# Reads of turned rows and of x, cut into 128-partition transfers instead of 32-partition ones, in a fused adaptive-layer-norm transformer block

## The chip, the cores and the metric

The kernel runs on one core of a Trainium2 chip. The metric is the device time of one execution in microseconds (us). Before the change it is 3508.1 us, the median of three runs (3507.44 to 3511.53). The engines are named as in the profile: PE is TensorE, PEld its weight loads, DVE is VectorE, ACT is ScalarE, POOL is GpSimd, SP is SyncE, which here issues nearly all DMA transfers.

## The reference

All tensors are float32. For each of 8 batch elements, x has 1024 tokens of 512 values. Causal attention with 16 heads of 32 values is followed by a GELU layer of 2048, both with a modulation that depends on a condition vector:

```
mod = silu(cond) @ Wada + bada                       # 6 rows of 512 per batch element
sh_a, sc_a, gt_a, sh_m, sc_m, gt_m = split(mod, 6)
xm = layernorm(x, g1, be1) * (1 + sc_a) + sh_a
x  = x + gt_a * (causal_attention(xm, Wqkv) @ Wproj + bproj)
xm = layernorm(x, g2, be2) * (1 + sc_m) + sh_m
x  = x + gt_m * (gelu(xm @ W1 + b1) @ W2 + b2)
```

What the change touches lies between the layer norm and the first product after it: the normalized rows (tokens in the partitions) have to be turned, so that the 512 features lie in the partitions, because a product on TensorE sums over partitions.

## The kernel before

The 8192 tokens are worked on as 16 blocks of 512 tokens (two per batch element). Each block has a first stage (key `a0` to `a15`, normalization of x ahead of the projections to queries, keys and values) and a second stage (`m0` to `m15`, normalization ahead of the GELU layer). The products are cut by a Strassen scheme into seven half-size products over the parts B11, B21, B22 and T1 to T4 of the modulated, turned activations `xm` (`strassen`). Attention of one block is interleaved with projections and the GELU layer of others.

The order of the instructions on each engine is written out by the program itself: a planner keeps an estimated clock per engine (`now`) and due times of tiles (`written`, `left`), and picks at each step which thread of work advances. The cost that it books for a DMA is an argument of `note_dma`: 3600 ns for each transfer of x, 2600 ns for the write of a turned block to DRAM and 1250 ns for each read back. At run time the engines follow that fixed order, each in turn, and wait on semaphores. Transfers are all issued by SP in a fixed order: weight tiles of 256 KB into a ring of eight buffers (`fetch`, lines 358 to 362), x, residual rows, outputs, and the turn.

A turn happens in two ways. The keys in `by_pe` (a0, a1, m0, m1, m14, m15) are turned by TensorE, through transposes against an identity (line 764). The other 26 keys (a2 to a15 and m2 to m13) go through DRAM:

- `load_x` (lines 402 to 414) reads a block of x into the tile `hat_a`, 128 partitions by 4 by 512 values. For turned keys the token that stands in partition 32m + i at place a is token (4m + a) * 32 + i of the block. Four transfers of 256 KB fill the tile. `x` rows are 2 KB.
- `normalize` takes the statistics of each quarter `tiles[:, t, :]` (line 619) on DVE, a power on POOL, and applies mean and deviation to each quarter on ACT or DVE (lines 655 and 660).
- `turn` (lines 692 to 716) transposes 32 by 32 blocks of each quarter on DVE (line 700), with the modulated tile `xm` as a scratch place, writes this tile to DRAM as `held` in one transfer of 1 MB (line 709), waits for it, and reads it back in four transfers of 256 KB into the `hat` tile (lines 712 to 715), where now the features lie in the partitions.
- `modulated` (lines 721 to 789) then makes four chunks of `xm`, each from all four quarters `got[:, :, ts(c, P)]`, with a scale and a shift on ACT (line 774) or DVE (line 768), and the sums and differences T1 to T4 on DVE and POOL (lines 784 to 789 and 167, 170). TensorE's products read `xm_a`, `xm_m` and their sums `t_a`, `t_m` (line 217).

The same ACT queue holds the exponentials of the attention (line 1698) and evacuations of product banks (line 197); DVE holds the row maxima (line 1610) and the other evacuations (line 208).

Of the kernel before, what the change touches and what calls it, by code (L numbers as in the profile page):

```python
# [22 lines left out]
def kernel(  # L23
# [33 lines left out]
    nc = tc.nc  # L57
    B, T, D = x.shape
    HD = W1.shape[1]
    P = 128  # L60
    hd = D // H
    scale = float(hd) ** -0.5
    TB = 512
    NTT = TB // P
# [48 lines left out]
    def note(engine, ns, reads=(), writes=(), port=False):  # L113
        start = max(now[engine], due(reads, writes))
        if port:
            start = max([start] + [b for a, b in pool_spans if a <= start < b])
        end = start + ns
        now[engine] = end
        if engine == "POOL":
            pool_spans.append((start, end))  # L120
            del pool_spans[:-16]
        for k in reads:
            left[k] = max(left.get(k, 0.0), end + SYNC)
        for k in writes:
            written[k] = end + SYNC
        return end

    def note_dma(ns, reads=(), writes=(), after=0.0):

        begun = max(now["SP"], due(reads, ()), after)  # L130
        now["SP"] = begun + ISSUE
        now["DMA"] = max(begun + BEGIN, now["DMA"]) + ns
        for k in writes:
            written[k] = now["DMA"] + LAND
# [108 lines left out]
    def mlp_steps(n):  # L243
        return [("u", n, i) for i in range(NQ)] + [("d", n, part) for part in range(4)]
# [9 lines left out]
    for w in range(1, NB):  # L254
        n = w - 1
        m = mlp_steps(n)
# [132 lines left out]
    rows = tmp.tile([P, TB], F32, tag="y", name="rows")[:n_rows, :P]  # L389
# [8 lines left out]
    Q = P // NTT  # L398

    def hat_tile(key):  # L400
        return tmp.tile([P, NTT, D], F32, tag="hat", name=f"hat_{key}", bufs=1)

    def load_x(n):
        b, h = blocks[n]
        rows = hat_tile(f"a{n}")
        written["hat free"] = NEVER
        for t in range(NTT):
            some = x[b, h * TB + t * P : h * TB + (t + 1) * P, :]
            if f"a{n}" in by_pe:
                nc.sync.dma_start(rows[:, t, :], some)  # L410
            else:
                nc.sync.dma_start(rows[ts(t, Q), :, :], some.rearrange("(t i) d -> i t d", i=Q))
            note_dma(3600, [], [("x", f"a{n}")])
        return rows

    x_pre = {0: load_x(0)}
    fetch()

# [134 lines left out]
    def add_job(job, reads, first=False):  # L553

        at = sum(1 for other in jobs if other[2]) if first else len(jobs)
        jobs.insert(at, (job, reads, first))
# [135 lines left out]
    def turn(key, rows, xm):  # L692

        small_blocks = xm.rearrange("p c n -> p (c n)")
        by_tile = small_blocks.rearrange("p (m h t i) -> p h m t i", m=NTT, h=NC, t=NTT)
        written["blocks", key] = NEVER

        def turn_tile(t):
            into = by_tile[:, :, :, t, :]
            nc.vector.transpose(into, rows[:, t, :].rearrange("p (h m i) -> p h m i", m=NTT, i=Q))  # L700
            done = [("blocks", key)] if t == NTT - 1 else []
            note("DVE", 620, [("hat", key, t)], done)

        for t in range(NTT):
            add_job(lambda t=t: turn_tile(t), [("hat", key, t)], key[0] == "m")
        yield [("blocks", key)], []
        held = kept.tile([P, NTT * D], F32, tag=f"held_{turns[0] % 2}", name=f"held_{key}")
        turns[0] += 1
        nc.sync.dma_start(held, small_blocks)
        note_dma(2600, [("blocks", key)], [("held", key)])  # L710
        yield [("held", key)], []
        for m in range(NTT):
            some = held[:, ts(m, D)].rearrange("(a i) d -> i a d", i=Q)
            nc.sync.dma_start(rows[ts(m, Q), :, :], some)
            note_dma(1250, [("held", key)], [("turned", key)])
        yield [("turned", key)], []

# [3 lines left out]
    def modulated(key, gain, shift, b, guards):  # L721
# [23 lines left out]
        if turned:  # L745
            yield from turn(key, got, xm)
# [590 lines left out]
    def perform(step):  # L1337
# [7 lines left out]
        elif kind == "columns_m":  # L1345
            columns_of["m"] = norm_columns("m", 3, 4, O_G2, O_BE2)
        elif kind == "load_xa":
            x_pre[step[1]] = load_x(step[1])
        elif kind == "load_xr":
            start(load_xr(step[1]))  # L1350
# [643 lines left out]
```

## Time and profile before

| | us |
|---|---|
| median of three runs | 3508.1 |
| the profiled execution, its own time | 3510.74 |
| its span, from the first to the last instruction | 3509.0 |
| PE busy | 3454.3 (98%) |
| DVE busy | 2198.9 (63%) |
| POOL busy | 2084.2 (59%) |
| ACT busy | 1212.4 (35%) |
| DMA, queue of SP, share of 16 engines | 47.1% |

The granted clock of the profiled execution is 0.998. The profile is of one execution; an instruction is listed by its line in the kernel, its engine, what it writes and reads (out<-in, buffer numbers left out), its shape as partitions x elements, and a count. "Idle before" is the time that the engine stood still just ahead of such instructions, followed by what ended most of it. A row of the chain tells the share of the span by what the end of the work hung on, followed backwards. A DMA queue is listed with its packets, megabytes and the share of the 16 DMA engines' time that the packets took. In a table of stretches, the DMA share is the mean over the 16 engines, and a share a little over 1 comes from packets being booked to the stretch in which they start.

### The profile page before, as it was taken

Reading aid. Unit: us, or ns where it says so; the run is one execution under the profiler, and the core shown is the slowest. Engines: PE = TensorE matmul, PEld = TensorE weight load, DVE = VectorE, ACT = ScalarE, POOL = GpSimd, SP = SyncE. Lnnn points to the kernel's source line nnn. Section 1 sums busy time; section 2 is a strip of 40 time slices with the busy share of each in tenths; the row PEclk is TensorE's granted clock in tenths of the full one; section 3 lists DMA queues with packets and bytes.
Section 4 is the critical chain, followed back from the end, with each engine's and each line's share of the span. In section 5 each row is a group of like instructions: output and inputs, shape, how many; then the busy total and the mean of one; then the engine's idle time right before and its main releaser. Section 6 shows DMA issues by size and latency. Waiting matters only on the chain.

```text
span 3509.0 us, 120365 instructions
## 1 busy us (share of the span) xinstructions
PE 3454.3 (98%) x54429; PEld 1724.0 (49%) x54429; DVE 2198.9 (63%) x2401; ACT 1212.4 (35%) x1276; POOL 2084.2 (59%) x2258
## 2 busy tenths in 40 slices
PE   8999999999999999999999999999999999999999
PEld 4444445445554545445454454544555444554445
DVE  5766676564666656665666566765666756656563
ACT  2335333342233423335223342333423343232531
POOL 3767846666366663756727576275753658537660
PEclk9999999999999999999999999999999999999999
DMA  6843444535545445363454534545354544443334
GB/s 212 263 137 104 137 115 140 142 107 159 142 125 156 119 147 153 119 170 115 137 157 130 155 117 144 150 137 148 116 155 137 165 122 146 128 136 101 96 121 140
DMA packets 328194, 491.10 MB, mean 140 GB/s; under 512 B 27260, under 2 KB 177596, under 8 KB 324100
## 3 DMA queue, kind: packets, MB, share of 16 engines
q1 hardware_dynamic: 327568, 483.39, 47.1%
q8 instruction: 428, 7.01, 0.8%
q14 instruction: 82, 0.67, 0.1%
q10 hardware_dynamic: 116, 0.03, 0.0%
HBM read 425.57 MB, written 55.64 MB: 137 GB/s over the span
## 4 chain that ended last, share of the span: by engine, by line
PE 83%; POOL 7%; DMA 3%; DVE 3%; ACT 1%; issue 1%; SPq 1%; ACTq 0%; DVEq 0%; POOLq 0%
PE bank L217 59%; PE sc L1595 8%; PE st L1686 6%; PE po L1726 6%; POOL pT L1816 4%; PE st L1674 2%; PE bank L1747 2%; DMA hat_m<-held_m 1%; DVE mx L1610 1%; POOL hT L170 1%; ACT pT L1698 1%; DMA held_m<-xm_m 1%; PE bank L1648 0%; POOL xr L170 0%; DMA w<-in_L_cond_Wqkv_dram 0%
## 5 line engine op out<-in xcount | busy, mean ns | idle before, releaser
L1816 POOL TENSOR_TENSOR pT<-pT,pT 128x256 f32<-128x256 f32 (+3 forms) x1254 | 1219.7, 1007 | 298.5 <-PE po L1726 181.6
L1698 ACT ACTIVATE pT<-st 128x2048 f32<-128x2048 f32 x288 | 540.9, 1878 | 1065.1 <-PE st L1686 959.8
L217 PE MATMUL bank<-w,hT 128*32 128x256 f32 x14336 | 823.7, 380 | 0.4 <-issue 0.4
L1610 DVE TENSOR_REDUCE mx<-sc 128x4 f32<-128x2048 f32 (+3 forms) x384 | 665.9, 1755 | 235.6 <-PE sc L1595 229.5
L217 PEld LDWEIGHTS bank<-w,hT 128*32 128x32 f32 x14336 | 446.7, 110 | 390.3 <-issue 105.8
L217 PE MATMUL bank<-xm_m,w 128*32 128x256 f32 x8192 | 498.6, 381 | 3.6 <-ACT xm_m L774 2.2
L217 PE MATMUL bank<-t_m,w 128*32 128x256 f32 x6144 | 382.4, 380 | 0.9 <-DVE t_m L786 0.6
L217 PEld LDWEIGHTS bank<-xm_m,w 128*32 128x32 f32 x8192 | 255.6, 110 | 231.2 <-issue 62.2
L1703 POOL TENSOR_SCALAR_AFFINE_SELECT pT<-pT 128x512 f32<-128x512 f32 x256 | 167.5, 672 | 331.9 <-ACT pT L1698 329.4
L1607 DVE TENSOR_TENSOR sc<-sc,mask 128x1024 f32<-128x1024 f32 (+1 forms) x160 | 162.8, 1018 | 293.3 <-PE sc L1595 237.8
L1595 PE MATMUL sc<-kT,qT 32*128 32x512 f32 (+3 forms) x3072 | 329.5, 521 | 4.3 <-ACT pT L1698 3.3
L1726 PE MATMUL po<-pT,v 128*32 128x512 f32 (+3 forms) x3048 | 301.6, 490 | 3.9 <-POOL pT L1703 3.9
L1686 PE MATMUL st<-qT,kT 32*128 32x512 f32 (+3 forms) x3072 | 300.8, 487 | 0.0
L217 PEld LDWEIGHTS bank<-t_m,w 128*32 128x32 f32 x6144 | 189.6, 110 | 172.9 <-issue 48.5
L1765 DVE RECIPROCAL rec<-rec 128x128 f32<-128x128 f32 x256 | 227.3, 922 | 48.2 <-ACT rec L1756 48.2
L217 PE MATMUL bank<-xm_a,w 128*32 128x256 f32 x3968 | 243.4, 382 | 0.4 <-DMA w<-in_L_cond_Wqkv_dram 0.4
L217 PE MATMUL bank<-w,qT 128*32 128x512 f32 x2048 | 237.0, 595 | 1.1 <-DMA w<-in_L_cond_Wproj_dram 0.7
L1595 PEld LDWEIGHTS sc<-kT,qT 32*128 32x128 f32 x3072 | 129.6, 183 | 188.2 <-issue 88.4
L208 DVE TENSOR_TENSOR hT<-bank,u_u 128x512 f32<-128x512 f32 x187 | 126.6, 686 | 105.8 <-PE bank L217 103.1
L217 PE MATMUL bank<-t_a,w 128*32 128x256 f32 x2944 | 183.2, 380 | 0.0
L217 PEld LDWEIGHTS bank<-xm_a,w 128*32 128x32 f32 x3968 | 123.5, 110 | 110.3 <-issue 29.3
L1115 ACT ACTIVATE hT<-hT,cols 128x512 f32<-128x512 f32 x256 | 164.7, 712 | 35.9 <-DVE hT L208 28.5
(243 smaller groups left out, 3404.0 us busy)
## 6 DMA issues: line engine op xcount, KB each, us to landing
w<-in_L_cond_W_dram SPq DMA_DIRECT2D x384, 256.0 KB
w<-kept_up_S SPq DMA_DIRECT2D x256, 256.0 KB
w<-kept_down_S SPq DMA_DIRECT2D x256, 256.0 KB
w<-kept_qkv_S SPq DMA_DIRECT2D x180, 256.0 KB
w<-in_L_cond_Wqkv_dram SPq DMA_DIRECT2D x147, 256.0 KB
hat_a<-in_x_dram SPq DMA_DIRECT2D x64, 256.0 KB
xr<-in_x_dram SPq DMA_DIRECT2D x32, 512.0 KB
w<-in_L_cond_Wproj_dram SPq DMA_DIRECT2D x64, 256.0 KB
```

Of the source, the lines that this page charges most:

```text
L208: nc.vector.tensor_tensor(out, src, other, op)
L217: nc.tensor.matmul(ps[r, :], columns, rhs, start=start, stop=stop, skip_group_check=True)
L1115: nc.scalar.activation(hT[:, i, :], hT[:, i, :], AF.Gelu, bias=cols[:, O_B1 + f : O_B1 + f + 1])
L1595: nc.tensor.matmul(sc[:, j, c0 : c0 + w], qTs[n][r, gg, ts(qt, P)], keys_of(n, kh)[r, gg, :w], start=True, stop=True, skip_group_check=True,)
L1607: nc.vector.tensor_tensor(place, place, shape_of.to_broadcast(place.shape), ALU.add)
L1610: nc.vector.tensor_reduce(maxima[n, gg][:, kh, qt, :], sc[:, :, c0 : c0 + w], axis=AX.X, op=ALU.max)
L1686: nc.tensor.matmul(st[:, j, c0 : c0 + w], kT[r, gg, ts(k % NTT, P)], qT[r, gg, TB - w :], start=False, stop=True, skip_group_check=True,)
L1698: nc.scalar.activation(pT[:, :, :used], st[:, :, :used], AF.Exp, scale=scale)
L1703: nc.gpsimd.affine_select(diagonal, diagonal, pattern=[[0, HPG], [1, P]], compare_op=ALU.is_ge, fill=0.0, base=0, channel_multiplier=-1,)
L1726: nc.tensor.matmul(po[r, TB - w :], v[:, k % NTT, g * P + j * hd : g * P + (j + 1) * hd], pT[:, j, c0 : c0 + w], start=(k == 0), stop=last ...
L1765: nc.vector.reciprocal(some, some)
L1816: nc.gpsimd.tensor_tensor(into, into, pT[:, j, c0 : c0 + w], ALU.add)
```

## The change

Both the reads of x for turned keys and the reads of turned rows are cut along the other axis of the tile. The tile holds the same values in the same places afterwards, and there are as many transfers of the same size in the same order. Before, transfer t (or m) filled all four places in 32 partitions (four runs of 2 KB in each). Now transfer t (or a) fills one place, one run of 2 KB, in all 128 partitions. On the DRAM side a transfer of x took four runs of 32 consecutive rows that follow one another; now it takes four runs of 32 consecutive rows that are 128 rows apart. For the turned rows, the source was 2 KB from each of the 128 rows of `held`; now it is all 8 KB, in four pieces that go to four partitions, of each of 32 rows. The reads for a0 and a1 stay as they are. The planner's costs stay as they are too.

```diff
         for t in range(NTT):
-            some = x[b, h * TB + t * P : h * TB + (t + 1) * P, :]
             if f"a{n}" in by_pe:
-                nc.sync.dma_start(rows[:, t, :], some)
+                nc.sync.dma_start(rows[:, t, :], x[b, h * TB + t * P : h * TB + (t + 1) * P, :])
             else:
-                nc.sync.dma_start(rows[ts(t, Q), :, :], some.rearrange("(t i) d -> i t d", i=Q))
+                some = x[b, h * TB : (h + 1) * TB, :].rearrange("(m a i) d -> a m i d", a=NTT, i=Q)
+                nc.sync.dma_start(rows[:, t, :], some[t])
             note_dma(3600, [], [("x", f"a{n}")])
...
-        for m in range(NTT):
-            some = held[:, ts(m, D)].rearrange("(a i) d -> i a d", i=Q)
-            nc.sync.dma_start(rows[ts(m, Q), :, :], some)
+        for a in range(NTT):
+            some = held[ts(a, Q), :].rearrange("i (m d) -> m i d", m=NTT)
+            nc.sync.dma_start(rows[:, a, :], some)
             note_dma(1250, [("held", key)], [("turned", key)])
```

Here `P` is 128, `Q` is 32, `NTT` is 4, `D` and `TB` are 512.

## The prediction

> **What bounds the kernel now.** I read the page first: the busy times and the chain, then the DMA queues.
>
> ```profile
> span 3509.0 us, 120365 instructions
> ...
> PE 3454.3 (98%) x54429; PEld 1724.0 (49%) x54429; DVE 2198.9 (63%) x2401; ACT 1212.4 (35%) x1276; POOL 2084.2 (59%) x2258
> ...
> DMA packets 328194, 491.10 MB, mean 140 GB/s; under 512 B 27260, under 2 KB 177596, under 8 KB 324100
> ...
> q10 hardware_dynamic: 116, 0.03, 0.0%
> ...
> PE 83%; POOL 7%; DMA 3%; DVE 3%; ACT 1%; issue 1%; SPq 1%; ACTq 0%; DVEq 0%; POOLq 0%
> ```
>
> TensorE is busy in 98% of the span: 3509.0 less 3454.3 leaves 54.7 us of idle time in all. So a faster transfer can win little and a slower one can cost much, wherever TensorE ends up waiting for it. Next I read what TensorE waits for. The rows give us in total, times, and the longest.
>
> ```profile
> PE bank L217 <- ACT xm_m L774: 2.2, 2, 2.0
> ...
> PE bank L764 <- ACT xm_a L774: 1.2, 1, 1.2
> ...
> PE bank L217 <- DVE t_m L786: 0.6, 1, 0.6
> ```
>
> These are all the waits that hang on the modulated chunks, into which a turned read feeds: 2.2 + 1.2 + 0.6 = 4.0 us. Third, the stretch around one turn (the second-stage turn at 685 us), in order of time, SyncE's and ScalarE's rows:
>
> ```profile
> 685.01 2.43 SPq L714 DMA_DIRECT2D hat_m<-held_m  x4
> 687.49 0.43 SPq L360 DMA_DIRECT2D w<-kept_up_S  x1
> ```
>
> ```profile
> 687.96 1.88 ACT L1698 ACTIVATE pT<-st 128x2048 f32<-128x2048 f32 x1 [5.72 <-PE st L1686]
> ...
> 695.10 2.93 ACT L774 ACTIVATE xm_m<-hat_m,shiftm,gainm 128x512 f32<-128x512 f32 x4 [4.79 <-DMA hat_m<-held_m]
> 697.94 1.85 ACT L1698 ACTIVATE pT<-st 128x2048 f32<-128x2048 f32 x1
> ```
>
> ScalarE stands idle for 4.79 us until the four reads have landed, makes the four chunks, and only then runs the next exponential, which was queued behind them. So the read already ends last in this stretch, and a later landing delays the exponential too.
>
> **The change, part by part.** *Issues.* Number, place and size of all transfers stay: 104 turned reads and 56 reads of x, four to a group, 26 and 14 groups.
>
> ```profile
> w<-in_L_cond_W_dram SPq DMA_DIRECT2D x384, 256.0 KB
> w<-kept_up_S SPq DMA_DIRECT2D x256, 256.0 KB
> w<-kept_down_S SPq DMA_DIRECT2D x256, 256.0 KB
> w<-kept_qkv_S SPq DMA_DIRECT2D x180, 256.0 KB
> w<-in_L_cond_Wqkv_dram SPq DMA_DIRECT2D x147, 256.0 KB
> ...
> hat_a<-held_a SPq DMA_DIRECT2D x56, 256.0 KB
> ...
> hat_m<-held_m SPq DMA_DIRECT2D x48, 256.0 KB
> ```
>
> Each still moves 128 rows of 2 KB. The instruction order on every engine is the same, since the planner's costs for these transfers are untouched: it goes on assuming the old speed. Issue costs nothing more (0.6 us each, 2.43 for four), and no queue is passed.
>
> *Waits.* The statistics of x (line 619) wait for one transfer each in place of all four with the first. Worth nothing: the reads of x issued at 714.07 are first used here, 38 us later:
>
> ```profile
> 752.09 0.68 DVE L619 BATCH_NORM_STATS2 st_a<-hat_a 128x6 f32<-128x512 f32 x1
> ```
>
> The modulation (lines 768 and 774) reads all four quarters at once and waits for all four transfers, before and after.
>
> *The speed of a read.* Three stretches, with length, busy times of PE, PEld, DVE, ACT, POOL, then granted clock, DMA share, GB/s: weight loads of 2 KB rows, the turned read of above, a read of x.
>
> ```profile
> 684.00:685.50 1.50, 1.50 (x36) 0.90 (x32) 1.47 (x3) 0.00 (x0) 1.50 (x2) 1.00 0.89 341
> 688.00:692.50 4.50, 4.30 (x68) 1.61 (x64) 1.93 (x2) 2.32 (x2) 2.94 (x6) 1.00 1.06 203
> 717.00:719.50 2.50, 2.50 (x40) 1.05 (x36) 2.09 (x3) 0.00 (x0) 2.24 (x2) 1.00 1.07 220
> ```
>
> A busy DMA engine moves 341 / (0.89 x 16) = 23.9 GB/s in weight loads, which fill 128 partitions, and 203 / (1.06 x 16) = 12.0 in a turned read, where all 16 engines write into the same 32 partitions. A group of four (1.049 MB) takes 1.049 / 203 = 5.2 us now. That half rate is what the change goes after. On 16 engines at the fast rate a group would take 1.049 / 382 = 2.7 us.
>
> *How many engines.* The old source pattern runs over 32 rows, then 4 blocks; the new one over 4 blocks, then 32 rows, and the blocks can't be joined with the rows: their steps are 512 and 2,048 elements in the turned read, 65,536 and 512 in that of x. If a transfer is dealt to DMA engines by its outermost count, 32 can be dealt over 16 engines, 4 over no more than four. The scalar queue's loads at the start show how transfers with few rows are dealt:
>
> ```profile
> rows<-in_L_cond_g_dram ACTq DMA_DIRECT2D x2, 2.0 KB
> rows<-in_L_cond_be_dram ACTq DMA_DIRECT2D x2, 2.0 KB
> ...
> rows<-in_L_cond_bproj_dram ACTq DMA_DIRECT2D x1, 2.0 KB
> rows<-in_L_cond_b_dram ACTq DMA_DIRECT2D x1, 2.0 KB
> rows<-in_L_cond_b_dram ACTq DMA_DIRECT2D x1, 8.0 KB
> rows<-in_L_cond_bada_dram ACTq DMA_DIRECT2D x1, 12.0 KB
> ```
>
> They carry 32 KB in rows of 512 B, 64 packets, but the queue (q10) has 116. The other 52 are 6 x 4 + 16 + 12: one closing packet on each engine, four engines for a vector of 4 rows, 16 for 16 rows, 12 for 24. So the outermost count, or its largest divisor up to 16, sets the number. What the trace doesn't have is a transfer with 4 outermost on one side and 128 on the other. I take four, the count into which both sides can be cut alike.
>
> [...]
>
> *Price of a group on four engines.* Fast end: 1.049 MB / (4 x 23.9) = 11.0 us, 5.8 more than now. Slow end, if the four still hinder each other as 16 do now: 1.049 / (4 x 12.0) = 21.9 us, 16.7 more. [...] Neither row is nearer, so I take the middle, 16.4 us: 11 us more.
>
> [...]
>
> *What it meets.* (a) TensorE directly. For each of the 26 turns I took the time from the end of the second modulated chunk to the first product that reads that turn's chunks (the program's order tells which product belongs to which turn), from the instructions by tile. The first turn and the last:
>
> ```profile
> L217 PE MATMUL bank<-xm_a,w x44: 376/379/403, 151.9 to 156.0; 128*32 128x256 f32 x44
> ...
> L774 ACT ACTIVATE xm_a<-hat_a,shifta,gaina x4: 797/800/812, 150.1 to 152.2; 128x512 f32<-128x512 f32 x4
> ```
>
> ```profile
> L217 PE MATMUL bank<-xm_m,w x8: 379/391/403, 3065.1 to 3065.4; 128*32 128x256 f32 x8
> ...
> L768 DVE TENSOR_SCALAR xm_m<-hat_m,gainm,shiftm x1: 635/635/635, 3052.0 to 3052.0; 128x512 f32<-128x512 f32 x1
> ```
>
> That is 151.9 - 151.6 = 0.3 us and 3065.1 - 3052.6 = 12.5 us. Seven of the 26 have under 3 us: 0.3, 0, 0, 0, 2.9, 1.9, 2.2; the next are 9.7, 10.0, 10.1, 11.9, 12.5, the other fourteen 14 to 42. With 11 us more the seven lose 10.7 + 33 + 8.1 + 9.1 + 8.8 = 69.7 us (the three about 10 lose 3 more, which (b) holds already).
>
> (b) Through ScalarE and VectorE, where evacuations and exponentials are queued behind the waiting modulation. Two rows by tile (idle us before them, times), and the exponentials' group from the page (busy, mean ns | idle before):
>
> ```profile
>   DMA hat_m<-held_m: 35.5, 10
> ```
>
> ```profile
>   DMA hat_a<-held_a: 20.7, 9
> ```
>
> ```profile
> L1698 ACT ACTIVATE pT<-st 128x2048 f32<-128x2048 f32 x288 | 540.9, 1878 | 1065.1 <-PE st L1686 959.8
> ```
>
> At 10 + 9 = 19 turns an engine already stands idle for the read, so it has no cushion ahead. Behind it, an exponential has 1065.1 / 288 = 3.7 us of idle time before it, which I take as the cushion for what comes next. The 19 less the seven of (a) are 12 turns, each losing 11 - 3.7 = 7.3 us: 87.6 us.
>
> (c) Weights behind a group. They run on all 16 engines, so each waits for the four busy ones. The five rows of w above are 1,223 loads, one in 2.9 us; the ring of eight asks for a tile some seven tiles, 20 us, ahead. A group of 16.4 us fits into that: nothing. At 21.9 it doesn't, 1.9 us at each of 14 groups of x, 27 us. (d) The reads of x: 22 us against 38, nothing.
>
> *Sum.* 69.7 + 87.6 = 157 us on the profiled execution's 3510.7 (span 3509.0 and 1.7 around it), which stands 2.6 above the median 3508.1; I put the changed median at 3508 + 157 = 3665. Fast end: seven turns 5.5 + 17.4 + 2.9 + 3.9 + 3.6 = 33, and 12 x 2.1 = 25: 3566. Slow end: 16.4 + 50.1 + 13.8 + 14.8 + 14.5 = 110, 12 x 13 = 156, and 27: 3801.
>
> **The rivals.** *Still 16 engines* (the destination's 128 partitions decide): the group takes 2.7 us, 2.5 sooner, and TensorE gains at most the 4.0 us that it waits for the chunks: 3504. Not slower. For it speaks that 128 partitions is the shape of every fast load here; against it the 52 packets. It decides if more than eight engines share a read, for then a group takes under 5.5 us. *Four engines, mostly hidden*: the cushions behind ScalarE hold and only (a) at the fast end is left: 3541. For it speaks ScalarE's 35% busy share; against it the exponential at 697.94, already late. [...]
>
> **How the numbers follow.** Four engines as summed 0.73, mostly hidden 0.08, slow with weights 0.12, still 16 engines 0.07. The likeliest gives 3665, its own range the fast to the slow end, 3566 to 3801. The range 3540 to 3815 takes in the second and most of the third, and leaves out the fourth. A measurement tells 0.2% (7 us) from no change: the first three cases are slower, 0.92 with a little taken off for both signs of error; the fourth is same (0.05) or, if the exponentials gain too, faster (0.03).
>
> **What would show it.** In the changed profile: packets under 512 B fall from 27260 by 160 x 12 = 1920 to 25340 if each changed read has four closing packets; a stretch in a turned read moves 50 to 95 GB/s at a DMA share of a quarter; ScalarE's idle time for the turned reads rises from 35.5 + 20.7 to over 200 us; TensorE's waits for chunks, exponentials and evacuations rise by 157 us while its busy time stays. It is wrong if the packets stay at 27260, or if they fall and TensorE's waits don't grow.

## The result, and the profile after

The changed kernel takes 3685.9 us (median of five runs, 3679.8 to 3691.4), against 3507.8 for the kernel before in the same comparison. The ratio is 1.0506, with a 95% interval from 1.049 to 1.0521. It is 178 us slower.

The page of the changed kernel, the rows that answer to those shown of before:

```profile
span 3681.5 us, 120386 instructions
...
PE 3502.4 (95%) x54429; PEld 1738.2 (47%) x54429; DVE 2188.9 (59%) x2401; ACT 1212.2 (33%) x1276; POOL 2079.0 (56%) x2258
...
DMA packets 326275, 491.11 MB, mean 133 GB/s; under 512 B 25340, under 2 KB 175676, under 8 KB 322180
```

Two things stand here. The packets under 512 B fell from 27260 to 25340, which is 1920 = 160 x 12 to the packet: each of the 160 changed reads is closed on four engines instead of sixteen. And the span's 172.5 us more have two parts: TensorE's idle time went from 54.7 to 3681.5 - 3502.4 = 179.1 us (124.4 more), and its busy time grew by 48.1 us although it does the same work. The second part is not in the prediction; it is taken up below.

The same second-stage turn as before, now at 707 us (SyncE's row, then ScalarE's in order of time):

```profile
706.97 2.34 SPq L714 DMA_DIRECT2D hat_m<-held_m  x4
```

```profile
709.92 1.88 ACT L1698 ACTIVATE pT<-st 128x2048 f32<-128x2048 f32 x1 [5.72 <-PE st L1686]
...
722.20 2.93 ACT L774 ACTIVATE xm_m<-hat_m,shiftm,gainm 128x512 f32<-128x512 f32 x4 [9.93 <-DMA w<-kept_up_S]
725.03 1.85 ACT L1698 ACTIVATE pT<-st 128x2048 f32<-128x2048 f32 x1
```

From the first read's issue to the first chunk it was 695.10 - 685.01 = 10.1 us and is now 722.20 - 706.97 = 15.2. (The wait is put down to a weight load here; the chunk reads only `hat_m`. Such a row names what came last by the profile, and should not be read further.) Taken in the same way at all 26 turns, the mean went from 9.34 to 15.73 us: 6.4 us later. The exponential behind the chunks is again late, and so is TensorE:

```profile
717.72 0.61 PE L217 MATMUL bank<-t_a,w 128*32 128x256 f32 x8
723.06 3.21 PE L217 MATMUL bank<-xm_m,w 128*32 128x256 f32 x28 [4.73 <-ACT xm_m L774]
```

Two stretches with nothing but a turned read and a read of x on the DMA engines (length, busy times of PE, PEld, DVE, ACT, POOL, granted clock, DMA share, GB/s):

```profile
717.00:719.00 2.00, 1.34 (x24) 0.48 (x16) 0.00 (x0) 0.00 (x0) 1.62 (x4) 1.00 0.27 96
745.00:748.00 3.00, 3.00 (x48) 1.30 (x44) 2.26 (x3) 0.23 (x1) 2.41 (x2) 1.00 0.25 94
```

A quarter of the DMA engines moves 94 to 96 GB/s, 22 to 24 GB/s for each busy one (94 / (0.25 x 16) = 23.5). So each engine has about the rate of the weight loads, twice what it had in the old form, and there are a quarter as many: 203 GB/s became 96.

What TensorE waits for now (us in total, times, longest). The waits for the chunks themselves and their differences, 4.0 us before, are 38.1 us in all (26.5 and 9.2 below, and two of 1.3 and 1.1), and only a part of it:

```profile
PE st L1674 <- DVE mx L1610: 26.6, 10, 7.2
PE bank L217 <- ACT xm_m L774: 26.5, 5, 7.3
PE sc L1595 <- ACT pT L1698: 13.9, 4, 6.7
PE bank L217 <- DMA w<-in_L_cond_Wproj_dram: 10.6, 2, 6.6
PE bank L217 <- DVE xm_a L768: 9.2, 2, 4.7
PE bank L1648 <- DVE u_q L208: 7.3, 1, 7.3
PE bank L217 <- ACT qT L197: 7.2, 1, 7.2
```

Maxima, exponentials, evacuations: work that has nothing to do with the turned rows, but stands behind the modulation in the queues of ScalarE and VectorE.

TensorE's products stand in the same order in both kernels, so the loss can be read turn by turn: by how much the delay of one and the same product grows from the reads of one turn to those of the next. At 21 of the 26 turns 5.4 to 9.5 us are lost, at the other five 1.2 to 3.3.

### The profile page after: what moved, and what is told of

It reads as the page before. It is cut to its first block, busy times and chain, and to the rows that moved or that the text cites. A ratio compares the mean times of both kernels' runs of the same rounds, so it can differ in the third digit from the quotient of the medians.

```text
span 3681.5 us, 120386 instructions
## 1 busy us (share of the span) xinstructions
PE 3502.4 (95%) x54429; PEld 1738.2 (47%) x54429; DVE 2188.9 (59%) x2401; ACT 1212.2 (33%) x1276; POOL 2079.0 (56%) x2258
## 2 busy tenths in 40 slices
DMA packets 326275, 491.11 MB, mean 133 GB/s; under 512 B 25340, under 2 KB 175676, under 8 KB 322180
## 5 line engine op out<-in xcount | busy, mean ns | idle before, releaser
L217 PE MATMUL bank<-xm_m,w 128*32 128x256 f32 x8192 | 506.5, 385 | 34.5 <-ACT xm_m L774 26.5
L1595 PE MATMUL sc<-kT,qT 32*128 32x512 f32 (+3 forms) x3072 | 332.3, 525 | 15.2 <-ACT pT L1698 13.9
L217 PE MATMUL bank<-w,qT 128*32 128x512 f32 x2048 | 243.6, 608 | 16.6 <-DMA w<-in_L_cond_Wproj_dram 10.6
```

The source lines that it names most:

```text
L217: nc.tensor.matmul(ps[r, :], columns, rhs, start=start, stop=stop, skip_group_check=True)
L1595: nc.tensor.matmul(sc[:, j, c0 : c0 + w], qTs[n][r, gg, ts(qt, P)], keys_of(n, kh)[r, gg, :w], start=True, stop=True, skip_group_check=True,)
```

## The experiments

Theory A was that the turned reads land later and every turn pays for it. Against it stood theory B (few engines hold up the weights queued behind any changed read), and later the question what makes a late landing cost so much.

**The turned reads alone, and the reads of x alone.** Each run keeps one half of the change. The first:

```diff
-            nc.sync.dma_start(rows[:, t, :], some[t])              # x: as before the change
+            nc.sync.dma_start(rows[ts(t, Q), :, :], some.rearrange("(t i) d -> i t d", i=Q))
```

> Only the turned reads are cut into 128 partitions; the reads of x stay as before. Theory A (the loss is the later landing of the turned reads, 6.4 us at each of 26 turns, met by TensorE directly or through ScalarE and VectorE): 3670 to 3690 us, as with the whole change, TensorE idle time about 175 us. Theory B (the loss is four engines that hold up the weights queued behind any such group, of x or turned): the 26 turned groups of 40 carry 26/40 of 178 us, so about 3624 us. Both: packets under 512 B 27260 - 104 x 12 = 26012.

> Only the reads of x are cut into 128 partitions; the turned reads stay as before. Theory A: nothing waits for them, 3505 to 3515 us. Theory B: 14/40 of 178 us, about 3570 us, with TensorE waiting for weights. Both: packets under 512 B 27260 - 56 x 12 = 26588.

Measured: turned reads alone 3687.9 us (ratio 1.051, 1.0495 to 1.0524), reads of x alone 3514.2 us (1.0017, 1.0008 to 1.0026). Their packets, in this order:

```profile
DMA packets 326947, 491.11 MB, mean 133 GB/s; under 512 B 26012, under 2 KB 176348, under 8 KB 322852
```

```profile
DMA packets 327522, 491.10 MB, mean 140 GB/s; under 512 B 26588, under 2 KB 176924, under 8 KB 323428
```

Both counts are the expected ones, so both halves run on four engines; but nearly all of the cost is that of the turned reads. Theory B falls as the main cause: 56 reads of x on four engines cost 5.5 us in all, not 62. (The 5.5 us are clear of noise, but where they arise can't be seen: the profiled execution of that kernel has a span of 3509.7 us, as good as before.)

**The same rows in 128 partitions, on 16 engines.** If the change fails only by its engines, a transfer with 128 outermost on both sides should bring what it was after. The blocks of 32 features are chosen with a step of four ahead of the transpose, so that 128 consecutive pieces of 2 KB in `held` (32 of its rows) have the features in the right order:

```diff
-            nc.vector.transpose(into, rows[:, t, :].rearrange("p (h m i) -> p h m i", m=NTT, i=Q))
+            nc.vector.transpose(into, rows[:, t, :].rearrange("p (h i m) -> p h m i", m=NTT, i=Q))
...
+            some = held[ts(a, Q), :].rearrange("i (m d) -> (i m) d", m=NTT)
+            nc.sync.dma_start(rows[:, a, :], some)
```

> The turned reads fill 128 partitions from 128 consecutive rows of the kept copy, so that both sides count 128 outermost; to keep the features in their places the transposes on VectorE take their 32 columns with a step of four. The reads of x stay as before. If the number of engines was the whole fault of the change: 16 engines again (packets under 512 B 27260), a turned read at the fast rate of 341 GB/s, a turn 2.5 us shorter than before (6.8 in place of 9.3 us), 3498 to 3508 us. Rival (the 128-partition form itself is at fault): slower than 3530 us. If transposes with a step cost VectorE more than 0.67 us: slower than 3508 us with longer transposes in the profile.

Measured: 3498.6 us, ratio 0.9971 (0.996 to 0.9982), faster than both kernels. The page's packet row, a stretch in a turned read, and the transposes by tile:

```profile
DMA packets 328195, 491.11 MB, mean 140 GB/s; under 512 B 27260, under 2 KB 177596, under 8 KB 324100
```

```profile
683.00:686.00 3.00, 2.82 (x40) 0.71 (x38) 0.63 (x1) 2.35 (x2) 1.47 (x4) 1.00 0.98 335
```

```profile
L700 DVE STREAM_TRANSPOSE xm_m<-hat_m x48: 1057/1150/1240, 666.1 to 3026.9; 128x512 f32<-128x512 f32 x48
```

All sixteen engines close each transfer again and move 335 GB/s. A turn takes 7.4 us instead of 9.3, and the 10 us gained come in spite of transposes that went from a median of 0.67 to 1.15 us. So 128 partitions are the better form here, and the change lost by the order of its source pattern.

**The reads of x in order as well.** They take 128 consecutive rows, as for a0 and a1, and the modulation puts tokens in order by writing runs of 32:

```diff
-                nc.sync.dma_start(rows[ts(t, Q), :, :], some.rearrange("(t i) d -> i t d", i=Q))
+                nc.sync.dma_start(rows[:, t, :], some)
...
-                out = xm[:, c, :].rearrange("p (a x) -> p a x", x=P)
+                out = xm[:, c, :].rearrange("p (t a x) -> p t a x", t=NTT, a=NTT)
```

> As the run with rows in order, and the reads of x for turned blocks take 128 consecutive rows as well; the modulation writes its chunk in runs of 32 in place of 128 to put tokens in order. Theory A: reads of x are hidden before and after, so within 3 us of the run with rows in order unless runs of 32 make the modulation longer than 0.80 us. Theory B: another gain of some us, since weights behind the reads of x come sooner.

Measured: 3498.6 us again, ratio 0.9972 (0.9962 to 0.9982). Faster reads of x gain nothing. A stretch in one of them:

```profile
711.00:713.00 2.00, 2.00 (x40) 1.04 (x32) 2.00 (x2) 0.00 (x0) 2.00 (x3) 1.00 0.88 296
```

In the kernel before, a read of the same 128 consecutive rows of x into 32 partitions moved 220 GB/s at a share of 1.07, which is 12.9 GB/s for each busy engine; into 128 partitions it is 296 / (0.88 x 16) = 21.0.

**Two engines.** The lateness is made larger, with two blocks outermost:

```diff
-            nc.sync.dma_start(rows[:, a, :], some)
+            for two in range(2):
+                nc.sync.dma_start(rows[half(two, 2 * Q), a, :], some[half(two, 2)])
```

> As the changed kernel, but each transfer is cut in two halves of 64 partitions, so that two blocks are outermost and, if the engines follow the outermost count, two engines carry each of eight transfers per group. Theory A (number of engines sets the landing, and every turn pays for it): packets under 512 B: 160 more transfers x 16, less 320 x 14, so 27260 + 2560 - 4480 = 25340; a group moves about 48 GB/s and takes 21.9 us, some 11 us more than on four engines, plus about 2 us for four more issues; each of 26 turns loses 11 to 13 us more, 3686 + 286 to 340 = 3970 to 4025 us, and weights come late behind a group (ring of 20 us), up to 100 us more. Rival (the loss is saturated, since planned order leaves other work behind the read): under 3850 us. If the two engines halve each other's rate as sixteen did before: over 4200 us.

Measured: 3954.4 us, ratio 1.1268 (1.1246 to 1.129), a little under the range expected for theory A. The busy row, the packet row, and a stretch with a turned read alone:

```profile
span 3954.8 us, 120571 instructions
...
PE 3513.0 (89%) x54429; PEld 1738.3 (44%) x54429; DVE 2182.0 (55%) x2401; ACT 1212.0 (31%) x1276; POOL 2075.3 (52%) x2258
...
DMA packets 326276, 491.11 MB, mean 124 GB/s; under 512 B 25340, under 2 KB 175676, under 8 KB 322180
```

```profile
746.00:749.00 3.00, 1.14 (x24) 0.47 (x16) 0.00 (x0) 0.00 (x0) 1.41 (x4) 1.00 0.13 49
```

Two of sixteen engines (share 0.13) move 49 GB/s, still 24 each, so they don't slow each other measurably. A turn takes 26.2 us, 16.9 more than before, and the kernel loses 444.4 us, 17.1 per turn. The rival with a saturating loss falls.

**Late on sixteen engines.** Is it lateness, or few engines? The kernel before, with each group preceded by four more reads of the same form, whose content is written over:

```diff
+        for m in range(NTT):
+            some = held[:, ts(m, D)].rearrange("(a i) d -> i a d", i=Q)
+            nc.sync.dma_start(xm[ts(m, Q), :, :], some)
         for m in range(NTT):
```

> The kernel before, on 16 engines and 32 partitions, with each group of turned reads preceded by four more of the same form into the modulated tile, which is written over afterwards: the wanted reads land a group (5.2 us) and up to 1.7 us of issue later, so a turn takes 14.5 to 16 us instead of 9.3, about as in the changed kernel (15.7), while no read runs on fewer than 16 engines. Theory A (lateness of the landing costs the time, whatever makes it late): 178 x 5.2 to 6.5 / 6.4 = 145 to 180 us, 3650 to 3690 us, with half clock after the stalls. Rival (reads on few engines cost by their own doing): under 3570 us.

Measured: 3641.1 us, ratio 1.038 (1.0361 to 1.0399). Its page:

```profile
span 3640.3 us, 120639 instructions
...
PE 3497.9 (96%) x54429; PEld 1735.0 (48%) x54429; DVE 2188.1 (60%) x2401; ACT 1212.6 (33%) x1276; POOL 2079.7 (57%) x2258
...
DMA packets 343174, 518.42 MB, mean 142 GB/s; under 512 B 28924, under 2 KB 179260, under 8 KB 339076
```

The packets are 27260 + 104 x 16: every extra read runs on sixteen engines. A turn takes 14.45 us, 5.1 more than before (just under the range expected), and the loss is 133.7 us, 5.1 per turn; the time expected, 3650 to 3690, was missed by 9 us in step with that. Put together (idle and busy time of TensorE from the spans and busy rows, against 54.7 and 3454.3 us before):

| kernel | a turn, us | later by | lost per turn, us | more idle time per turn | more busy time per turn |
|---|---|---|---|---|---|
| extra reads, 16 engines | 14.45 | 5.1 | 5.1 | 3.4 | 1.7 |
| the change, 4 engines | 15.73 | 6.4 | 6.9 | 4.8 | 1.9 |
| 2 engines | 26.2 | 16.9 | 17.1 | 14.9 | 2.3 |

Whatever makes it late, each microsecond of lateness costs about a microsecond, on average over the 26 turns, and few engines are not needed for it. But this is a sum of two things. The idle time grows by 1.6 to 2.0 us less than the lateness, so there is a cushion of that size per turn; and the longer busy time, taken up below, puts about as much on top. A part of the idle time, in these rows, is put down to weights queued behind the reads: 5.2 us before, and in the order of the table 31, 23 and 112 us. So what is late is not the turned block alone, and theory B keeps a minor share that these runs don't separate.

**The planner told.** Is the cushion so small because the order of the instructions was fixed with the old landing in mind? One number of the changed kernel is altered:

```diff
-            note_dma(1250, [("held", key)], [("turned", key)])
+            note_dma(2850, [("held", key)], [("turned", key)])
```

> The changed kernel with one number more changed: the planner books 2850 ns instead of 1250 ns for each turned read, which is 1250 + (15.7 - 9.3) us / 4 by the measured turns, so it may put other work ahead of what waits. Theory A (loss is in-order queues that expect the old landing): most of the 178 us comes back, 3520 to 3590 us, at turns as long as in the changed kernel (15.7 us). Rival (the four engines' slowness itself, through weights or DMA load, costs the time): over 3640 us.

Measured: 3571.0 us, ratio 1.0169 (1.0151 to 1.0187), with turns as long as in the change (15.9 us). Its busy row:

```profile
PE 3477.4 (97%) x54429; PEld 1733.3 (49%) x54429; DVE 2236.3 (63%) x2434; ACT 1201.8 (34%) x1260; POOL 2080.6 (58%) x2244
```

115 of the 178 us come back with no transfer faster. So most of the loss hangs on the order: on what stands in a queue behind a late wait.

**TensorE kept busy.** The busy time rose by 48 us. Spare products, whose result nothing reads, are put ahead of the modulation at 24 turns:

```diff
+            if turned and c == 0 and bank_at() < now["PE"]:
+                spare = lin_bank()
+                for _ in range(16):
+                    nc.tensor.matmul(
+                        banks[spare][:hd, :P], ident[:, :hd], ident, start=True, stop=True, skip_group_check=True
+                    )
+                live[spare] = False
```

> The changed kernel with 16 spare products of 32 columns, whose result nothing reads, on TensorE ahead of the place where the modulation of a turned block is put, at 24 of 26 turns, some 4 us each. If the halved clock after each stall costs 48 us (busy time 3502 against 3454 us before) and idle time of over about 3 us brings it on: granted clock back near 0.998, the spare products fall into stalls of about 5 us, and the time is about 3640 us. Rival (the clock fall costs nothing of its own, or the stall stands elsewhere): 3686 us or up to 96 us more.

Measured: 3660.4 us, ratio 1.0428 (1.0411 to 1.0444), granted clock 0.993 (0.978 in the change); between the 3640 us expected and the 3686 of the rival. Its busy row, and the spare products' group (busy, mean ns | idle before):

```profile
PE 3551.5 (97%) x55197; PEld 1815.8 (50%) x55197; DVE 2185.9 (60%) x2401; ACT 1212.4 (33%) x1276; POOL 2078.6 (57%) x2258
```

```profile
L769 PE MATMUL bank<-ident 128*32 128x128 f32 x768 | 87.9, 273 | 0.0
```

The ends of the spare products' records overlap other products by 12.6 us: all others together are busy for 3476.2 us, 26.2 less than in the change for the same work. (Without the overlap it would be 3551.5 - 87.9 = 3463.6.) The rest of the span, 3655.6 - 3476.2 = 179.4 us, holds the idle time and the spare products, and the change had 179.1 us of idle time: the spare products fell into stalls, and the 25.9 us between the spans are shorter busy time. A kernel with more work for TensorE is faster than the one without it; the clock costs time of its own.

**Rows in order, and the planner told of it.**

```diff
-            note("DVE", 620, [("hat", key, t)], done)
+            note("DVE", 1100, [("hat", key, t)], done)
...
-            note_dma(1250, [("held", key)], [("turned", key)])
+            note_dma(775, [("held", key)], [("turned", key)])
```

> The kernel with turned rows in order, with the planner's costs set to what its run showed: 775 ns for each turned read and 1100 ns for each transpose with a step of four (it booked 1250 and 620). Theory A: the waits on the turn were small already, so within 10 us of 3498.6 us to either side. If the planner can use the 2 us sooner: under 3490 us.

Measured: 3509.5 us, ratio 0.9999 (0.999 to 1.0008): 11 us slower than with the old costs, just outside what was expected, though a turn is still 7.0 us. So costs nearer to the measured ones don't make a better order by themselves. Two costs were changed at once, reads shorter by 4 x 475 ns and transposes longer by 4 x 480; which of them did it is not shown.

## Why the prediction was right, and where its working was not

The forecast was 3665 us (157 us more), the measured time is 178 us more, inside the range and near the point. Step by step:

*Four engines.* Right, to the packet. The scalar queue's first loads (6 x 4 + 16 + 12 closing packets) told how transfers are dealt, and the changed kernels show the mixed case that was missing: the counts 25340, 26012 and 26588 are those of four closing packets for each read with 4 outermost on one side and 128 on the other.

*The price of a group.* This step failed: "I take the middle, 16.4 us: 11 us more". The measured rate is near that of the fast end, 22 to 24 GB/s per engine, on four engines and on two, and a turn is 6.4 us longer. No run shows a group at 16.4 us, nor four engines at the half rate of the slow end, from which the 3801 us of slow weights come: four engines moved 94 to 96 GB/s, 10.9 to 11.2 us for a group of 1.049 MB. Engines with 32 partitions each did not slow each other measurably (a busy engine moved 23.9 GB/s in the weight loads). The half rate before goes with sixteen engines inside the same 32: the same rows of x moved at 12.9 GB/s per busy engine into 32 partitions and at 21.0 into 128.

*(a) and (b), what it meets.* With 6.4 us the seven direct turns would give 6.1 + 19.2 + 3.5 + 4.5 + 4.2 = 37.5 us and the twelve others 12 x (6.4 - 3.7) = 32 us, 70 in all. Idle time grew by 124 us. Turn by turn, the seven took 32 us of it, so (a) was about right. The step that failed is (b), "3.7 us of idle time before it, which I take as the cushion", with "12 turns": nineteen others, not twelve, took 88 us, 4.6 each. The cushion that the three late kernels show is 1.6 to 2.0 us per turn. Why the mean idle time before an exponential is no such reserve is argued and not shown: most of it, 959.8 of 1065.1 us, is ScalarE waiting for TensorE, which is itself held up by what stands behind the modulation. (The remaining 4.5 us of idle time arise ahead of the first turn.)

*What was not in the sum.* The busy time, expected to stay, rose by 48 us. So a lateness taken too large made up for a cushion taken too large, turns left out and a clock that wasn't thought of. That the total came out near 178 is luck; its direction and the path through the queues are not.

*The signs.* The packets, the rate and the share of the DMA engines came as said. ScalarE's and VectorE's idle time put down to the turned reads rose from 35.5 + 20.7 to 51.5 + 85.4 = 137 us, not to over 200; a part of these waits is now put down to weight loads, as at 722 us above, so this sign can't be read cleanly. TensorE's idle time rose by 124 us, not by 157, and its busy time did not stay.

*(c) and (d).* Reads of x were nearly hidden, as said (5.5 us). The weights behind a group were not quite free: TensorE's waits for weights are 22.6 us against 5.2 (the largest, 10.6 us, stands among the rows above).

*The rivals.* Sixteen engines was the wrong case for this change, but its price was tried: it was put at 4.0 us at most and brought 10 us (where the rest comes from was not traced). "Mostly hidden" fell because the cushion is small.

## What to carry to other kernels

Look at a transfer's outermost count on both sides, not at the partitions that it covers: 128 partitions from a source with 4 outermost ran on 4 of 16 DMA engines, while as many bytes from 128 consecutive pieces ran on all, and the closing packets in the profile tell how many there were (12 fewer for each changed read). Where every engine follows an order fixed in advance, the mean idle time of an engine is no cushion for a late transfer whose consumer stands in its queue ahead of other work: here each late microsecond cost about one (5.1, 6.9 and 17.1 us for 5.1, 6.4 and 16.9), idle time and the slower clock behind it (0.50) together. When a transfer gets slower by intent, tell the planner: that alone gave back 115 of 178 us.

## What the runs showed of the hardware that was not expected

After most of these stalls the clock of TensorE halves, and it stays halved into the work that follows. Three neighbouring stretches of the changed kernel around the turn at 707 us (columns as above; the clock is the third number from the end):

```profile
713.00:720.00 7.00, 5.34 (x84) 2.42 (x84) 2.89 (x2) 0.00 (x0) 5.62 (x9) 1.00 0.60 168
720.80:727.60 6.80, 4.54 (x40) 1.72 (x40) 2.68 (x4) 5.16 (x6) 1.67 (x1) 0.50 0.12 42
728.00:735.00 7.00, 7.00 (x104) 3.12 (x100) 5.37 (x5) 2.85 (x4) 0.00 (x0) 1.00 0.22 73
```

TensorE stopped at 718.3; at 720.8 the granted clock fell to 0.50, and it came back 6.8 us later, although the products had gone on from 723.1. In those 4.5 us of work only 40 products ran, where 104 take 7.0 us at the full clock. Such falls stand at most of the 26 turns of the changed kernel, for 3.4, 6.8 or 10.2 us each, and 164 us in all; in the kernel before there are two within the work and one at its end, 17 us. In the changed kernel each of the 23 stalls of TensorE of 3.0 us and more was followed by such a fall, 2.0 to 4.9 us after its start, and so were three of the five of 2.4 to 3.0 us; in the kernel before, one of 3.1 us was not. TensorE was not always idle throughout just before: at 720.8 the clock fell 2.5 us after the stop, and in the 3.4 us ahead of the fall (the length of the shortest falls) TensorE had been busy for 28%, at others of this kernel for up to 41%. Over the whole trace TensorE worked at half rate for 109.8 us, against 10.9 in the kernel before; half of the 98.9 us more is 49.5, which is about the 48.1 us by which its busy time grew. So a stall of 5 us costs about 2 us more in the work behind it (48.1 us over some 24 stalls).
